# Attention and a grouped mixture of experts on one core: which 512 tokens go densely and when, sorting on GpSimd, results scattered by token

## The chip, the cores and the metric

One core of a Trainium2 chip runs the whole kernel. The time is device time in microseconds for one launch; the number compared is the median of several launches on the same chip. All arithmetic is in 32-bit floats, with small bf16 helpers. In the text the engines are called PE (TensorE, matmuls), DVE (VectorE), ACT (ScalarE), POOL (GpSimd) and SP (SyncE, which only issues DMAs here).

## The reference

Two batches of 1024 tokens, 128 features. First attention with latent keys and values, normed before and behind; then a mixture of experts, normed before and behind.

```
x = x + layernorm(attention(layernorm(x)))       # 8 heads, 2 latent kv heads of 32, causal
x = x + layernorm(ffn(layernorm(x)))

# ffn, per token h:
scores = sigmoid(h @ gate_weight.T)              # 32 experts in 4 groups of 8
sc     = scores + gate_bias
group_scores = top_k(sc.reshape(T, 4, 8), 2).sum(-1)
gidx   = top_k(group_scores, 2)                  # 2 of 4 groups stay open
topidx = top_k(sc where the group is open, 6)    # 6 experts
tw     = scores[topidx];  tw = tw / (sum + 1e-20) * 0.2
routed = sum over the 6 of tw * (silu(h @ w_gate[e]) * (h @ w_up[e])) @ w_down[e]
shared = (silu(h @ shared_w_gate) * (h @ shared_w_up)) @ shared_w_down
anchor = the same form with anchor topidx[:, 0] // 2
out    = routed + shared + 0.1 * anchor
```

Each token therefore needs 2 of the 4 groups; a group here holds 8 experts and 4 anchors and is computed as five chunks of 128 hidden columns.

## The kernel before

The 2048 tokens are four parts of 512: (batch 0, first half), (0, second), (1, first), (1, second). Three of them are sorted by group, so that only the two groups of each token are computed: their rows, 128 features and 48 weights (E + A), are written to the DRAM table `placed` at places given by `place_of`, in 15 slots of 256 rows (NS), of which each holds rows of one group. The fourth part, `dense`, goes through all four groups unsorted, with zero weights where a token has nothing to do with a group.

The sort has two sets. `place_first` (L971) covers the first two parts: `ranked` counts on PE how many earlier tokens chose each group, DVE works out the places (`slots_of`, `started`, `moved`), `numbers_of` (L949) reads the slots' group numbers into registers of PE and SP, and `move_rows` (L914) issues two indirect DMAs per tile of 128 tokens on POOL. `place_second` (L998) does it for the third part, which fills up what the first set left open.

All instructions stand in each engine's queue in the order in which the program writes them (`manual_schedule`), so an instruction that waits holds up everything behind it on its engine. Work beside the main line is written as generators: `tick()` (L251) advances one piece of each of the lists `ends`, `moves` and `side` by one step, and `yield HOP` makes a piece sit out two ticks. `attention()` ticks through its steps; `route` (L669), one generator for each part, does that part's output projection, the two norms, the router and the choice of groups and experts.

Behind attention comes `Slots.run` (L1146). For slot i and pair of chunks k it does `hidden` (gate and up matmuls, silu on ACT, two multiplies on DVE) and, two pairs later, `down`. At k = 0 it turns the rows of slot i+2 (`turn_rows`, L1067: four transposes, the weights written by ACT's queue to `cw_slot`) and fetches the weights of slot i+1; at k = 1 it fetches the rows of slot i+3 (L1062); at k = 2 the `spread` of slot i+2, the token weights of `cw_slot` broadcast over partitions (L1089, L1094). Weights, rows and spreads are all issued by SP, in this order. The result of a slot goes contiguously to `results` (L1141). When the slots are done, 24 indirect DMAs (`gather`, L1200) fetch the two results of each token, and `experts` (L1231) does the dense part, 20 chunks of 512 tokens, with `finish` (L1210: shared expert, sum, last norm, output) of the three sorted parts beside it in the ticks.

The norms' reciprocal root is always exp(-0.5 ln v) on ACT (`root`, L335) with a Newton step on DVE, and the router's sigmoid is a table of its own on ACT (L740), so that ACT loads tables at each change.

Of the kernel before, what the change touches and what calls it, by code (L numbers as in the profile page):

```python
# [17 lines left out]
P = 128  # L18
# [7 lines left out]
def attn_moe_block(  # L26
# [67 lines left out]

    sparse, dense = [(0, 0, TB), (0, TB, TB), (1, 0, TB)], [(1, TB, TB)]
    NT0 = 2 * TB
    NTS = sum(n for _, _, n in sparse)
    NS = TOPG * NTS * P // SL + NG - 1
    KS = NT0 * P // SL
    NS0 = -(-(TOPG * NT0 * P - NG * (SL - 1)) // SL)  # L100

# [66 lines left out]
    placed = dram.tile([NS * SL, D + E + A], F32, name="placed")  # L168
    results = dram.tile([NS * SL, D], F32, name="results")
    cw_slots = [dram.tile([E + A, SL], F32, name=f"cw_slot{i}") for i in range(NS)]  # L170
    cw_rows = {b: dram.tile([E + A, n * P], F32, name=f"cw_rows{b}") for b, _, n in dense}
# [8 lines left out]
    nc.gpsimd.memset(eps_t, EPS)  # L180
    ident_bf = const.tile([P, P], BF16, name="ident_bf")
# [29 lines left out]
    full = const.tile([P, NG, KS], F32, name="full")  # L211
    for k in range(KS):
        nc.gpsimd.memset(full[:, :, k], float(k * SL))
    number = const.tile([P, NS], F32, name="number")
    for i in range(NS):
# [3 lines left out]
    nc.gpsimd.memset(zero, 0.0)  # L219

# [4 lines left out]
    step_by = step_by.rearrange("p k g -> p (k g)")  # L225
    nc.sync.dma_start(
        out=placed.rearrange("(k p) c -> p k c", p=P),
        in_=zero.unsqueeze(1).to_broadcast([P, NS * JL, D + E + A]),
    )

# [17 lines left out]
    wakes, now = {}, 0  # L248
    HOP = 2

    def tick():  # L251
        nonlocal now
        now += 1
        for queue in (ends, moves, side):
            for piece in list(queue):
                if wakes.get(piece, 0) > now:
                    continue
                gap = next(piece, queue)
                if gap is queue:
                    queue.remove(piece)  # L260
                elif gap != 0:
                    wakes[piece] = now + (gap or 1)
                    break
# [57 lines left out]
    class Norm:  # L321
        def __init__(self, n, name):
            self.n = n
            for k, shape in (("st", [P, n, 6]), ("mv", [P, n, 2]), ("r0", [P, n]), ("t", [P, n]),
# [10 lines left out]
        def root(self):  # L335

            tables(EXP_LN)
# [3 lines left out]
        def newton(self):  # L341

# [4 lines left out]
            nc.vector.tensor_tensor(self.rs, r0, t, ALU.mult)  # L347

        def apply(self, dst, src, i):
            nc.vector.tensor_scalar(  # L350
                dst, src, self.mv[:, i, 0:1], self.rs[:, i : i + 1], ALU.subtract, ALU.mult
            )

        def negated(self):
            nc.vector.scalar_tensor_tensor(
                self.nb, self.mv[:, :, 0], -1.0, self.rs, ALU.mult, ALU.mult
# [23 lines left out]
    def project(b, c):  # L380
# [6 lines left out]
        yield  # L387
        if b:
            yield
        norm.root()  # L390
        yield
        norm.newton()
        if b:
            norm.negated()
            yield
        for i, t in enumerate(tiles):
            (norm.apply_act if b else norm.apply)(xn[:, i, :], x_sb[b][:, t, :], i)
        yield
        xnT = work.tile([P, BC], F32, tag="xnT", name=f"xnT{b}{c}")
        transposed(xn, xnT, f"xn{b}{c}")  # L400
        yield
# [261 lines left out]
    routed = {}  # L663
# [5 lines left out]
    def route(b, t0, n):  # L669


        name = f"{b}{t0}"
# [4 lines left out]
        sorts = (b, t0, n) in sparse  # L677
        assert n == TB
# [16 lines left out]
        norm.root()  # L695
        yield HOP
        norm.newton()
        norm.negated()
        yield HOP
# [9 lines left out]
        norm.root()  # L709
        yield HOP  # L710
        norm.newton()
        norm.negated()
        yield HOP
        if sorts:
            row = rows[b, t0] = const.tile([P, n, D + E + A], F32, name=f"rows{name}")
# [6 lines left out]
        yield HOP + 1  # L722
# [16 lines left out]
        loaded[0] = None  # L739
        nc.scalar.activation(score.rearrange("p t e -> p (t e)"), pl[:, 0 : n * E], AF.Sigmoid)  # L740
        yield HOP
        sc = scratch("sc", [E])
# [28 lines left out]
        if sorts:  # L771
            at = sum(p[2] for p in sparse[: sparse.index((b, t0, n))])
            own = chosen[:, at : at + n, :]
        else:
            own = gm
# [51 lines left out]
        if not sorts:  # L827
# [6 lines left out]
            nc.sync.dma_start(out=cw_rows[b], in_=cwT)  # L834
            yield
        routed[b, t0] = True
# [5 lines left out]


# [531 lines left out]
```

## Time and profile before

| | us |
|---|---|
| median of 4 launches | 508.68 (504.35 to 510.44) |
| the profiled launch | 507.35 |
| its span, first to last instruction | 505.6 |

| engine | busy us | share of the span | instructions |
|---|---|---|---|
| PE, matmuls | 429.2 | 85% | 3727 |
| DVE | 298.3 | 59% | 1046 |
| ACT | 222.0 | 44% | 464 |
| POOL | 83.7 | 17% | 160 |

The shares are means over stages that differ: attention, the slots, the dense part with the finishing of the others, and a tail. A line of the groups or of the timeline gives the engine, the line of the kernel, what is written and read with its partitions and elements, and a duration; what stands in brackets is the idle time of that engine just before, and what ended it. "issue" and "remote" are waits for which the profile finds no instruction or DMA of this kernel. The granted clock is PE's, as a share of full speed. An instruction that issues a DMA is charged to its queue (SPq, ACTq), not to the transfer.

### The profile page before, as it was taken

The numbers are of one execution on the slowest core, as the hardware profiler recorded it, in microseconds if no ns is written. First come the engines' busy times: TensorE is split into PE (matmuls) and PEld (weight loads), VectorE is DVE, ScalarE is ACT, GpSimd is POOL, SyncE is SP. The second block draws the span as 40 slices with busy tenths as digits, with TensorE's granted clock in tenths as the row PEclk, the third lists the DMA queues.
The fourth block names the chain that finished last, engine by engine and source line by source line (L and its number), as shares of the span: only waits on it lengthen the run. The fifth ranks groups of instructions, "written<-read, shape, count | busy, mean of one in ns | idle before, by whom it ended". The sixth has DMA issues, their size and how long they took to land.

```text
span 505.6 us, 10160 instructions
## 1 busy us (share of the span) xinstructions
PE 429.2 (85%) x3727; PEld 264.9 (52%) x3727; DVE 298.3 (59%) x1046; ACT 222.0 (44%) x464; POOL 83.7 (17%) x160
## 2 busy tenths in 40 slices
PE   8998979999889999859687479589989999937990
PEld 5554544545445556424334368578879874413430
DVE  4579563786967986986304554344665445416882
ACT  3445654566426765425436125434433222122442
POOL 3000000021001201003831005200000005750010
PEclk9999998999989999988759777899999999968996
DMA  8990000000000000001120725576677684624230
GB/s 221 209 273 10 2 1 2 1 2 3 2 1 2 3 1 1 2 1 67 66 80 8 218 90 161 146 210 212 186 239 223 194 272 113 162 64 134 60 89 21
DMA packets 42946, 47.45 MB, mean 94 GB/s; under 512 B 17392, under 2 KB 35936, under 8 KB 42896
## 3 DMA queue, kind: packets, MB, share of 16 engines
q1 hardware_dynamic: 37520, 39.81, 27.6%
q0 software_dynamic: 1920, 3.74, 2.5%
q10 hardware_dynamic: 3456, 3.25, 2.0%
q8 instruction: 30, 0.49, 0.4%
q14 instruction: 20, 0.16, 0.1%
HBM read 38.06 MB, written 11.34 MB: 98 GB/s over the span
## 4 chain that ended last, share of the span: by engine, by line
PE 46%; DVE 25%; issue 7%; DMA 6%; ACT 5%; POOL 4%; SPq 3%; another core or an unknown queue 1%; ACTq 0%; POOLq 0%; DVEq 0%
DVE nm L471 9%; DMA wbs<-wgu 5%; PE sm L454 5%; PE s L519 4%; PE pgs L1111 4%; PE ys L1134 4%; PE o L556 4%; PE pus L1111 3%; PE pp L407 3%; POOL placed L921 3%; PE o L565 3%; SPq L1094 2%; PE pg L1264 2%; PE pu L1265 2%; PE po L685 2%
## 5 line engine op out<-in xcount | busy, mean ns | idle before, releaser
L471 DVE TENSOR_REDUCE nm<-sm 128x1 f32<-128x512 f32 (+2 forms) x192 | 92.6, 548 | 47.3 <-PE sm L464 24.8
L539 ACT ACTIVATE pr<-s 128x512 f32<-128x512 f32 (+1 forms) x160 | 75.7, 558 | 81.0 <-PE s L533 72.0
L519 PE MATMUL s<-qT,kT 32*128 32x256 f32 (+1 forms) x640 | 54.0, 396 | 10.7 <-DVE pos L901 6.3
L519 PEld LDWEIGHTS s<-qT,kT 32*128 32x128 f32 x640 | 35.2, 190 | 28.6 <-issue 16.2
L1119 DVE TENSOR_TENSOR hids<-hids,pus 128x512 f32<-128x512 f32 x30 | 20.6, 687 | 49.6 <-PE pus L1111 38.6
L542 POOL TENSOR_SCALAR_AFFINE_SELECT pr<-pr 128x1024 f32<-128x1024 f32 x16 | 18.1, 1128 | 185.7 <-ACT pr L539 185.7
L556 PE MATMUL o<-pr,v 128*32 128x256 f32 (+1 forms) x640 | 43.1, 390 | 5.3 <-issue 3.9
L454 PE MATMUL sm<-kT,qT 32*128 32x512 f32 (+3 forms) x384 | 45.8, 533 | 1.5 <-DVE nm L471 1.2
L1134 PEld LDWEIGHTS ys<-wd_sb,hids 128*128 128x128 f32 x300 | 41.8, 199 | 5.3 <-DVE hids L1120 1.6
L565 PE MATMUL o<-pr,ones 128*32 128x256 f32 (+1 forms) x640 | 43.1, 369 | 1.6 <-issue 1.5
L1134 PE MATMUL ys<-wd_sb,hids 128*128 x300 | 42.5, 284 | 1.8 <-DVE hids L1120 1.2
L1203 POOL DMA_INDIRECT y<-results,place_of x24 | 23.0, 958 | 108.7 <-PE pu L1265 101.7
L1111 PE MATMUL pgs<-hTp,wbs 128*128 128x256 f32 x120 | 34.3, 412 | 7.7 <-DMA wbs<-wgu 5.5
L1118 ACT ACTIVATE hids<-pgs 128x512 f32<-128x512 f32 x30 | 17.9, 598 | 34.8 <-PE pgs L1111 34.7
L1111 PE MATMUL pus<-hTp,wbs 128*128 128x256 f32 x120 | 32.3, 393 | 0.0
L921 POOL DMA_INDIRECT placed<-rows,place_of x24 | 23.7, 989 | 51.2 <-DVE place_of L911 47.1
L556 PEld LDWEIGHTS o<-pr,v 128*32 128x32 f32 x640 | 17.5, 114 | 28.0 <-issue 18.2
L1268 ACT ACTIVATE hid<-pg 128x512 f32<-128x512 f32 x20 | 11.8, 597 | 46.0 <-PE pg L1264 25.7
L1269 DVE TENSOR_TENSOR hid<-hid,pu 128x512 f32<-128x512 f32 x20 | 13.7, 683 | 28.9 <-PE pu L1265 13.1
L565 PEld LDWEIGHTS o<-pr,ones 128*32 128x32 f32 x640 | 17.5, 110 | 24.6 <-issue 15.5
L1278 PE MATMUL oacc<-hid,wd_sb 128*128 128x512 f32 x40 | 21.8, 627 | 9.5 <-DVE hid L1270 9.5
L1120 DVE TENSOR_TENSOR hids<-hids,spreads 128x512 f32<-128x512 f32 (+1 forms) x45 | 27.1, 603 | 3.4 <-DMA spreads<-cw_slot 1.9
(270 smaller groups left out, 640.7 us busy)
## 6 DMA issues: line engine op xcount, KB each, us to landing
wbs<-wgu SPq DMA_DIRECT2D x15, 640.0 KB
spreads<-cw_slot SPq DMA_DIRECT2D x30, 256.0 KB
spreadd<-cw_rows SPq DMA_DIRECT2D x16, 256.0 KB
placed<-zero SPq DMA_DIRECT2D x1, 2640.0 KB
got<-placed SPq DMA_DIRECT2D x15, 176.0 KB
wbd<-wgu SPq DMA_DIRECT2D x4, 640.0 KB
spreads<-cw_slot SPq DMA_DIRECT2D x60, 32.0 KB
results<-ys ACTq DMA_DIRECT2D x15, 128.0 KB
```

What stands on the lines that cost most here:

```text
L454: nc.tensor.matmul(banks[r][:, at : at + k1 - k0], lhsT=qT[ts(r, L), g, ts(qt, P)], rhs=kT[ts(r, L), g, k0:k1], start=(at == 0), stop=Fals ...
L471: nc.vector.tensor_reduce(nm[:, k0 // BC, j, r : r + 1], banks[r][:, at : at + k1 - k0], AX.X, ALU.max, negate=True,)
L519: nc.tensor.matmul(banks[r][:, at : at + n], lhsT=kT[rows, g, ts(kt, P)], rhs=qT[rows, g, q * QC + lo : q * QC + lo + n], start=(i == 0), ...
L539: nc.scalar.activation(pr[:, r, 0:m], banks[r][:, 0:m], AF.Exp)
L556: nc.tensor.matmul(o[ts(r, L), lo : lo + n], lhsT=qkv[b][2][:, kt, ts(g, L)], rhs=pr[:, r, at : at + n], start=(kt == 0), stop=False, skip ...
L565: nc.tensor.matmul(o[ts(r, L), QC + lo : QC + lo + n], lhsT=ones32, rhs=pr[:, r, at : at + n], start=False, stop=True, skip_group_check=True,)
L921: move = nc.gpsimd.indirect_dma_start(out=placed[:, :], out_offset=bass.IndirectOffsetOnAxis(ap=place_of[:, k, i : i + 1], axis=0), in_=ro ...
L1111: nc.tensor.matmul(p[:, lo : lo + SL], lhsT=wb[:, m, ts(c, P)], rhs=hT, start=(lo == 0), stop=(c == pair[-1]), skip_group_check=True,)
L1120: nc.vector.tensor_tensor(hid[:, 0:n], hid[:, 0:n], sp[:, pair[0] : pair[-1] + 1, :].rearrange("p c t -> p (c t)"), ALU.mult,)
L1134: nc.tensor.matmul(o[:, ts(j, D)], lhsT=hid[:, at : at + P], rhs=w, start=(c == 0 and j == 0), stop=(c == NC - 1), skip_group_check=True,)
L1203: nc.gpsimd.indirect_dma_start(out=y[k][:, t, :], out_offset=None, in_=results[:, :], in_offset=bass.IndirectOffsetOnAxis(ap=place_of[:, k ...
L1278: nc.tensor.matmul(oacc, lhsT=wd_sb[:, c, :], rhs=hid, start=False, stop=(c == NG * NC - 1))
```

## The change

- The dense part is now the first part (batch 0, first half). It runs right behind attention, ahead of the slots. Parts 2 and 3 are the first set of the sort, part 4 the second.
- `place_first`, the first fetches of rows, the route of the last part and `place_second` are put on the list only when attention is over, and `tick` may then advance two side pieces at once (`at_once`). The first set's work thus runs beside the dense part.
- The arithmetic of the places moves from DVE to POOL, as more and smaller instructions (`more_than`, `in_turn`, `moved`). Registers with group numbers are now read by PE, SP and POOL.
- Each row in `placed` carries four more numbers: for each group, the row of `results` where this token's result for it belongs (twice the token's number, plus how many of its groups came before). Places that no token fills get spare rows. A slot's result is scattered to these rows by two indirect DMAs on POOL, and the 24 gathers give way to one plain read for each part (`finish`), in which a token's two results stand side by side.
- In `Slots.run` the rows of slot i+3 are fetched at k = 2, behind the spread of slot i+2, no longer at k = 1.
- `finish` of parts 2 to 4 runs beside the slots; the last one has to wait for the last slot. Parts 2 and 3 wait for 11 slots (NB0).
- Outside attention the norms' roots are taken on POOL with `pow` (`root_pool`); in attention the router's sigmoid is made from exp, so that ACT keeps its table.

The diff, cut to its core:

```diff
-    sparse, dense = [(0, 0, TB), (0, TB, TB), (1, 0, TB)], [(1, TB, TB)]
+    parts = [(b, t, TB) for b in range(B) for t in range(0, NT, TB)]
+    ND = 1
+    sets = [parts[1:3], parts[3:]]
+    NB0 = TOPG * NT0 * P // SL + NG - 1
+    ROW = D + E + A + NG
...
-    results = dram.tile([NS * SL, D], F32, name="results")
+    results = dram.tile([NTS * P * TOPG + NS * SL, D], F32, name="results")
...
+    nc.sync.dma_start(out=by_place[:, :, D + E + A : ROW], in_=spare)
...
-        for queue in (ends, moves, side):
+        for queue, most in ((ends, 1), (moves, 1), (side, at_once[0])):
...
+        def roots(self):
+            if loaded[0] == EXP_LN:
+                self.root_act()
+                yield HOP
+                self.newton()
+            else:
+                self.root_pool()
+            yield HOP
...
+        def root_pool(self):
+            eng, v, t, r0 = nc.gpsimd, self.v, self.t, self.r0
+            eng.tensor_scalar(v, self.var, EPS, None, ALU.add)
+            eng.tensor_tensor(r0, v, minus_half.to_broadcast([P, self.n]), ALU.pow)
...
+        if in_attention:
+            nc.scalar.activation(flat, pl[:, 0 : n * E], AF.Exp, scale=-1.0)
...
+        if sorts:
+            below = preceded[:, at : at + n, :]
...
+            nc.gpsimd.tensor_tensor(
+                row[:, :, D + E + A : ROW], below,
+                token_row[:, at : at + n].unsqueeze(2).to_broadcast([P, n, NG]), ALU.add,
+            )
...
+    def more_than(dst, x, n):
+        t = tiny("more", [P, NG])
+        eng.tensor_scalar(dst, x, 0.0, None, ALU.is_gt)
+        for k in range(1, n):
+            eng.tensor_scalar(t, x, float(k * SL), None, ALU.is_gt)
+            eng.tensor_tensor(dst, dst, t, ALU.add)
+
+    def in_turn(start, first, n):
+        eng.tensor_copy(start, first)
+        for d in range(1, NG):
+            eng.tensor_tensor(start[:, d:NG], start[:, d:NG], n[:, 0 : NG - d], ALU.add)
...
     def place_first():
...
+        more_than(full, far, NT0 * P // SL)
+        more_than(new, total, NT0 * P // SL)
...
+        in_turn(starts[:, 0, :], nslots.to_broadcast([P, NG]), full)
...
+        in_turn(starts[:, 1, :], nslots.to_broadcast([P, NG]), new)
...
+        moved(0, NT0, rank, "a")
         moves.append(move_rows(0, NT0, "first"))
+        routed.add(("first", "placed"))
+        yield HOP + 1
+        yield from numbered(0, NS0)
...
         def begin(self):
-            while "first" not in routed:
+            while ("first", "moved") not in routed:
                 yield 0
-            self.fetch_weights(0)
             for i in range(3):
                 self.fetch_rows(i)
...
+            while "experts fetched" not in routed:
+                yield 0
+            self.fetch_weights(0)
...
         def turn_rows(self, i):
...
+            nc.gpsimd.tensor_copy(
+                self.to_row[i].unsqueeze(2), got[:, :, D + E + A : ROW][:, :, bass.ds(self.groups[i], 1)]
+            )
...
         def down(self, i, k, hid):
...
                 nc.scalar.copy(y, o[:, 0 : JL * D])
-                nc.scalar.dma_start(
-                    out=results[ts(i, SL), :].rearrange("(p j) d -> p j d", j=JL),
...
+                for j in range(JL):
+                    nc.gpsimd.memset(between, 0.0)
+                    move = nc.gpsimd.indirect_dma_start(
+                        out=results[:, :],
+                        out_offset=bass.IndirectOffsetOnAxis(ap=self.to_row[i][:, j : j + 1], axis=0),
+                        in_=y[:, ts(j, D)], in_offset=None,
+                    )
...
         def run(self):
...
                     if k == 0:
                         self.turn_rows(i + 2)
                         self.fetch_weights(i + 1)
-                    if k == 1:
-                        while NS0 <= i + 3 < NS and "second" not in routed:
-                            tick()
-                        self.fetch_rows(i + 3)
                     if k == 2:
                         self.fetch_spread(i + 2)
+                        self.fetch_rows(i + 3)
-                    for _ in range(1 if "second" in routed else 3):
+                    for _ in range(3):
                         tick()
...
+    def finish(i):
...
+        while some.done < (NS if last else NB0):
+            yield 0
...
+        nc.sync.dma_start(
+            out=both.rearrange("p (t c) -> p t c", t=n),
+            in_=results[0 : NTS * P * TOPG, :].rearrange("(t p k) d -> p t (k d)", p=P, k=TOPG)[
+                :, at : at + n, :
+            ],
+        )
...
-    some = Slots()
-    side += [*(route(*part) for part in sparse[:2]), place_first(), some.begin()]
-    side += [*(route(*part) for part in sparse[2:]), place_second()]
-    side += [route(*part) for part in dense]
-    attention()
-    some.run()
-    for b, t0, n in dense:
...
+    side += [route(i) for i in range(len(parts) - 1)]
+    attention()
+    at_once[0] = 2
+    some = Slots()
+    side += [place_first(), some.begin(), route(len(parts) - 1), place_second()]
+    experts(0, 0)
+    side += [finish(i) for i in range(ND, len(parts))]
+    some.run()
```

## The prediction

> **What bounds the kernel now.** I read the page's slices first, then a table by stage, then the waits, then the timeline of two places. The slices (each digit a fortieth of the span, in tenths) show TensorE (PE) near full in attention and ragged behind it, with the granted clock falling there.
>
> ```profile
> PE   8998979999889999859687479589989999937990
> PEclk9999998999989999988759777899999999968996
> ```
>
> By stage (window, its length, then busy time and count of PE, weight loads, DVE, ACT, POOL; granted clock, DMA share, GB/s):
>
> ```profile
> 220.50:226.70 6.20, 0.00 (x0) 0.00 (x0) 5.44 (x30) 1.42 (x3) 0.00 (x0) 0.77 0.00 0
> ...
> 246.70:266.00 19.30, 13.21 (x82) 5.14 (x80) 1.19 (x3) 6.42 (x13) 9.58 (x17) 0.56 0.23 76
> ...
> 273.00:337.10 64.10, 45.01 (x229) 38.53 (x229) 29.43 (x120) 25.92 (x55) 10.29 (x21) 0.84 0.51 151
> 337.10:415.50 78.40, 74.32 (x469) 68.28 (x470) 44.67 (x131) 28.88 (x62) 0.00 (x0) 1.00 0.73 217
> 415.50:493.40 77.90, 65.02 (x154) 27.96 (x153) 43.96 (x98) 23.77 (x38) 26.79 (x27) 0.91 0.39 109
> 493.40:505.60 12.20, 0.66 (x4) 0.42 (x4) 2.92 (x16) 2.95 (x5) 1.26 (x1) 0.64 0.07 22
> ```
>
> Attention ends at 273, the 15 slots at 415.5, the dense part at 493.4; 12.2 us of tail follow. PE sets the time where it is fed, and it is not fed in four places: 220.5 to 226.7, 246.7 to 266, the first slots, and parts of the dense stage. The waits (total us, times, longest):
>
> ```profile
> ACT pr L539 <- remote: 7.9, 2, 7.1
> ...
> DVE hid L1269 <- remote: 7.4, 1, 7.4
> ...
> PE s L519 <- DVE pos L901: 6.3, 1, 6.3
> ```
>
> The last one is the hole at 220.5: PE's queue holds the register loads of `numbers_of` (L950), which need DVE's 30 small instructions of `place_first`. The two "remote" waits lie at 251 and 443, each while POOL issues indirect DMAs back to back (twelve from 242.9, then 24 gathers from 421.5); PE, ACT and DVE stand together with no releaser in the kernel.
>
> **The change, part by part.** *Attention.* `place_first` and its 16 moves leave it. Gone: the 6.2 us hole, and in 246.7 to 266 the difference between 19.3 us and 13.21 us at clock 0.56 (7.4 us of full-clock work), 11.9 us; some 2 us of clock lost behind the first hole (20 us at 0.90) too. One unit more of routing is moved in (four transposes and a copy for the dense part, five small POOL instructions for each sorted one): 1 us. Sum -19: attention ends at 254. If the 11.9 us have another cause than the moves, it is 266.
>
> *Dense part, now first.* The same 20 chunks: PE starts pairs of L1264 at 423.45 and 426.03, so 20 x 2.57 = 51.4, plus 2.1 for the shared matmuls (1.02 + 1.12) and 2 for the last two chunks: 55.5. The 24 gathers and the 8.5 us that PE stood in them (442.9 to 451.4) are gone. Its weights and first spreads have nothing before them on SP and load during attention. Beside it runs now the sorting, on POOL. I count 35 + 15 = 50 small POOL instructions in `place_first` (`more_than` twice 7, `in_turn` twice 4), then 16 moves, 27 small ones and 8 moves in `place_second`, and 16 in the two `root_pool` of the last part's route. Of POOL (group, busy us, mean ns) the trace shows:
>
> ```profile
> L921 POOL DMA_INDIRECT placed<-rows,place_of x24 | 23.7, 989 | 51.2 <-DVE place_of L911 47.1 <-issue 3.8
> ...
> L920 POOL MEMSET between<- 128x1 f32 x24 | 2.7, 112 | 0.0
> ...
> L201 POOL TENSOR_TENSOR rep<-rep,ident 128x32 f32<-128x32 f32 x2 | 0.5, 242 | 0.0
> ```
>
> The 128x4 arithmetic is not in it, nor `pow`: between 0.11 (a memset) and 0.24 us each; I take 0.20, nearer to the only arithmetic. A move costs 0.99 + 0.11 + 0.19 of issue = 1.27 us. From the end of attention: the third part's route ends some 6 ticks in, at 1.29 us each (two in a chunk) behind 4 us of start, and five ticks later the counts are there: 18. Then 50 x 0.20 = 10, 16 x 1.27 = 20.3, the route's own POOL work of 5 (two adds of 0.73, 16 root steps, memsets): 53. Rows back (2.4), turned, cut to `cw_slot` and spread (6 to 8): a first slot at 62 to 64. So POOL's chain (63) is longer than PE's work (55.5). POOL is in order: the last route's adds and roots queue behind the moves, ACT and DVE wait for them, and behind those stand the silu and the multiplies of the chunks. SP waits for the last move with later spreads queued behind it. I add 6 to the 63 for that and for a standstill as at 443 (8.5 us of PE), of which part falls into waits that exist anyway, and 1.3 for registers (225.4 to 226.7 before): 70, against 77.9 before. Ends: 57 (all hidden) and 85 (both standstills and all waits in series).
>
> A rule speaks against this: the Trainium skill, "GPSIMD Engine Reference", section 4.1, sends elementwise work to VectorE and calls GpSimd about twice as slow for two inputs. The 128x4 multiply of DVE (L347) took 0.162 us, and by that rule the 50 would cost 0.32 each and the stage 6 us more: 487 instead of 481.
>
> *The slots.* One edit decides here. `fetch_rows(i+3)` moves on SP from before `fetch_spread(i+2)` to behind it. That spread needs `cw_slot`, which needs the rows of i+2 turned. SP waited for just this:
>
> ```profile
> SPq L1089 <- DMA cw_slot<-cwTs: 39.0, 11, 16.2
> ```
>
> One round in the timeline (start, us, engine, line):
>
> ```profile
> 333.03 0.38 PE L1072 MATMUL pt_s<-ident,got 128*128 128x128 f32 x2
> ...
> 333.67 0.36 ACT L1078 COPY cwTs<-pt_s 48x256 f32<-48x256 f32 x1 [1.59 <-PE pt_s L1074]
> ...
> 334.06 0.32 ACTq L1079 DMA_DIRECT2D cw_slot<-cwTs  x1
> ...
> 335.76 1.16 SPq L1089 DMA_DIRECT2D spreads<-cw_slot  x2
> ...
> 337.12 2.36 SPq L1094 DMA_DIRECT2D spreads<-cw_slot  x4
> ...
> 339.73 0.40 SPq L1025 DMA_DIRECT2D wbs<-wgu  x1
> ...
> 340.92 0.42 SPq L1062 DMA_DIRECT2D got<-placed  x1
> ```
>
> And what a row read takes when somebody waits for it:
>
> ```profile
> 320.88 0.35 SPq L1062 DMA_DIRECT2D got<-placed  x1
> ...
> 323.24 0.69 PE L1072 MATMUL pt_s<-ident,got 128*128 128x128 f32 x2 [5.24 <-DMA got<-placed]
> ```
>
> Before, rows(i+3) did not wait for spread(i+2), so the round (turn, copy, `cw_slot`, spread, rows, turn) had two slots to close. After it has one: turn to `cw_slot` issue 1.03, landing 1.70 here (3.9 at 341.78 with weights in flight), spread issue 3.5 to 3.7, row read 2.36, 0.2 of gaps: 8.8 to 11.2. Weights are issued right behind the rows, 3.4 us ahead of the next `cw_slot`, so I take a landing of 2.3: 9.5 us a slot. Before, the copies L1140 at 351.87 and 412.44 are eight slots apart, 7.57 each; PE's own work is some 7.0. From slot 2's turn (2.9 into the slots) to slot 14's: 12 x 9.5 = 114, and 17.6 of PE behind it: 134.5, against 142.4 (415.5 - 273). The shared matmuls of `finish` (3 x 2.2) fit into PE's gaps of 2.5. Two scatters a slot are 2.5 us of POOL in 9.5, hidden; the second set's places are ready near slot 2, where rows(5) ask for them: 0 to 4, inside the round.
>
> *Tail.* From the last matmul: copy 0.5, two scatters 2.4, landing 1.5 (257.81 to 259.29 at the first rows), the read of both results 4.3 (640 KB of weights took 5.0), two adds 1.4, statistics 1.25, roots 1.7, applying 1.0, add 0.7, the output 5.1 (500.5 to 505.6): 20 against 12.2. The dense part's own tail is covered by slots now.
>
> *The rest* costs nothing seen: the 16-byte spare columns are written in the first 45 us and read after 254; `to_row` is one POOL copy a slot; the sigmoid from exp saves two table loads of 1.28 us on ACT in attention, where PE sets the pace.
>
> Sum: 254 + 70 + 134.5 + 20 = 478.5, +1.75 around the span (507.35 - 505.6) = 480; the median of 508.68 is 1.3 above the profiled run, so **481**.
>
> **Rivals.** *The row round does not close late* (turns find their rows): 7.5 x 15 = 112.5 in place of 134.5, 459. For it: in the trace only one turn ever waited for rows. Against: there rows ran a slot ahead. *The round is longer*: `cw_slot` lands in 3.9 as at 341.78, or PE's gap passes some 3 us and the clock drops, as behind the 3.5 us gap at 299.6 (not behind 2.2 at 274): 11.2 a slot, +20, 501. *The standstill at 246.7 was not the moves'*: attention ends at 266, 492. *Slower: POOL is the bound.* If a small POOL instruction costs 1 us (`pow` and 128x4 are unseen), the 50 put 40 us in front of the first slot, the roots 13 more, the second set 10 in the slots: some 530 with part hidden; it decides from 0.6 us each, where the 27 us gained are used up.
>
> **How the numbers follow.** Forecast 0.38 (its own range 466 to 495), rows on time 0.17, standstill stays 0.09, longer round 0.18 (half of it below 503.6), POOL the bound 0.18. A measurement here tells 1% from nothing, so faster (below 503.6) is 0.38 + 0.17 + 0.09 + 0.09 = 0.73, within 0.08 + 0.02 = 0.10, slower 0.17. 452 to 517 leaves out 0.04 of the fast case and most of the slow one.
>
> **What would show it.** Right: attention over near 254 without the hole at 220; from the third slot on PE waits for `got` before each turn, with slots 9 to 10 us apart and SP's rows behind its spreads; a tail near 20. Wrong: slots 7.5 apart; PE standing in the dense part behind POOL for over 20 us; POOL instructions of 128x4 far above 0.24.

## The result, and the profile after

The changed kernel takes 507.65 us (median of 42 runs, 502.53 to 510.81), the kernel before 507.36 (63 runs, 502.83 to 518.59). The ratio is 1.0006 with an interval of 0.9987 to 1.0024: no difference. The profiled execution after is 510.93 us with a span of 509.2, 0.6% above the median. Ratios and intervals leave out runs over 1.5% above the fastest of the same kernel, which medians keep; the traces of the changed kernel (510.93), of the moves apart (524.16) and of the reads on POOL (486.46) are of such runs.

One thing has to be known for every number below. The kernel before has two times. In three of the five sets of runs made for the experiments (kernels run one after the other on one chip; four chips in all, sets 1 and 2 on the same one) it took 508 us, as in the comparison above; in the other two it took 478 and 481, without exception within a set. The changed kernel took 508 to 509 in a set of either kind. Beside a kernel before of 481 us the change is 6% slower.

The slices of the page, PE's busy share and the granted clock in fortieths of the span, show no hole towards the end of attention, where before has two (220.5 and 246.7). There is one in slice 23, in the dense part (PE at 3), and a hollow in slices 27 to 29, where the slots begin, with the clock at 6 in slice 29:

```profile
PE   8998899998799999997999379976797978788760
PEclk9997999999799999999999779998688989899885
```

The table by stage (window, length, busy time and count of PE, weight loads, DVE, ACT, POOL; clock, DMA share, GB/s): attention, the dense part, the slots up to the copy of slot 3's result out of PSUM (slots counted from 0), the other slots, the tail.

```profile
0.00:254.00 254.00, 235.04 (x2868) 127.27 (x2869) 179.15 (x687) 132.03 (x298) 30.19 (x91) 0.97 0.19 48
254.00:330.70 76.70, 64.17 (x175) 29.25 (x176) 39.73 (x132) 26.17 (x46) 41.84 (x120) 0.91 0.41 118
330.70:395.30 64.60, 49.15 (x232) 40.62 (x231) 21.30 (x45) 16.98 (x38) 24.08 (x62) 0.84 0.46 135
395.30:491.90 96.60, 80.52 (x456) 71.46 (x454) 44.88 (x90) 26.97 (x62) 32.62 (x67) 0.93 0.59 173
491.90:509.20 17.30, 0.00 (x0) 0.00 (x0) 4.56 (x18) 3.04 (x6) 2.19 (x5) 0.64 0.17 57
```

Set against the forecast's sum, in its own terms:

| term | forecast | measured |
|---|---|---|
| attention ends | 254 | 254.0 |
| dense part | 70 | 76.7 |
| to slot 2's turn | 2.9 | 1.6 |
| slot 2's turn to slot 14's, 12 rounds | 114 | 134.3 |
| from there to the last copy | 17.6 | 25.3 |
| tail | 20 | 17.3 |
| span | 478.5 | 509.2 |

The turns of slots 2, 6 and 14 stand in the timeline of PE:

```profile
332.30 0.38 PE L1113 MATMUL pt_s<-ident,got 128*128 128x128 f32 x2
...
390.74 0.68 PE L1113 MATMUL pt_s<-ident,got 128*128 128x128 f32 x2 [3.05 <-DMA got<-placed]
...
466.58 0.44 PE L1113 MATMUL pt_s<-ident,got 128*128 128x128 f32 x2 [2.47 <-DMA got<-placed]
```

The first four rounds took 58.4 us where 38 were forecast, the eight behind them 75.8 where 76 were. So the first four are 20.4 of the 30.7 us by which the sum was too small; the stretch behind the last turn is 7.7, the dense part 6.7, and the other terms give 4.2 back. Two more traces of the changed kernel (`c1_after` and `c2_after`, 508.07 and 508.45) have 56.5 and 56.8 for the four rounds, 76.5 and 75.3 for the eight. Slot 3's copy (395.3) falls near slot 6's turn, and is used below as another mark of where the beginning ends.

The waits between 254 and 331 (total us, times, longest):

```profile
DVE hid L1329 <- ACT hid L1328: 17.7, 3, 13.4
ACT an L398 <- POOL between L963: 13.0, 1, 13.0
...
PE oacc L1338 <- DVE hid L1330: 8.7, 2, 8.6
```

They are one chain, read from its second line: ACT's normalising step of the last route waits 13.0 us for POOL (the releaser shown, a memset, is what POOL does next after the root); the silu L1328 stands behind it on ACT, the multiply behind the silu, PE behind the multiply. The timeline of POOL (start, duration) shows what POOL was doing:

```profile
280.45 0.96 POOL L964 DMA_INDIRECT placed<-rows,place_of  x1 [0.19 <-issue]
281.49 0.23 POOL L383 TENSOR_SCALAR v_attn<-mv_attn 128x4 f32<-128x4 f32 x1
281.80 1.06 POOL L384 TENSOR_TENSOR r_attn<-v_attn,minus_half 128x4 f32<-128x4 f32 x1
...
284.07 0.20 POOL L389 TENSOR_TENSOR t_attn<-mv_attn,rs_attn 128x4 f32<-128x4 f32 x1
284.36 0.24 POOL L390 TENSOR_SCALAR nb_attn<-t_attn 128x4 f32<-128x4 f32 x1
```

The root came behind 15.6 us of place arithmetic (261.4 to 277.0) and three moves. In the slots' beginning the same happens with the dense part's own last norm, and SP is held as well (waits from 331 to 400):

```profile
ACT y L398 <- POOL between L963: 13.8, 1, 13.8
DVE y L393 <- POOL rs_out L388: 10.0, 1, 10.0
```

POOL itself was held up there. It did the place arithmetic of the second set (328.7 to 336.6) and three moves, and the fourth move waited for the row read of slot 3; the root came behind it, at 347.76:

```profile
345.24 0.96 POOL L964 DMA_INDIRECT placed<-rows,place_of  x1 [4.65 <-DMA got<-placed]
```

That read had itself waited for moves. SP's queue there: the row read of slot 3 leaves at 342.14, 2.3 us behind the end of the spread's issue, that of slot 4 at 361.95, 3.5 us behind.

```profile
337.54 2.27 SPq L1139 DMA_DIRECT2D spreads<-cw_slot  x4
342.14 0.35 SPq L1103 DMA_DIRECT2D got<-placed  x1
...
356.47 1.99 SPq L1139 DMA_DIRECT2D spreads<-cw_slot  x4
361.95 0.35 SPq L1103 DMA_DIRECT2D got<-placed  x1
```

In the steady slots the round runs as forecast; from slot 6 on the turns come 9.1 to 9.8 us apart. SP issues the spread, then the rows, and PE's turn waits for them; the next spread leaves only behind the turn:

```profile
414.12 1.99 SPq L1139 DMA_DIRECT2D spreads<-cw_slot  x4
416.21 0.36 SPq L1103 DMA_DIRECT2D got<-placed  x1
...
419.60 0.44 PE L1113 MATMUL pt_s<-ident,got 128*128 128x128 f32 x2 [0.74 <-DMA got<-placed]
...
422.38 1.16 SPq L1134 DMA_DIRECT2D spreads<-cw_slot  x2
```

These waits of PE over the whole run, before (total us, times, longest):

```profile
PE pt_s L1072 <- DMA got<-placed: 5.2, 1, 5.2
```

and after:

```profile
PE pt_s L1113 <- DMA got<-placed: 20.3, 11, 3.3
```

### The profile page after: what moved, and what is told of

The parts are those of the page before. It is cut to its first block, busy times and chain, and to the rows that moved or that the text cites. A ratio compares the mean times of both kernels' runs of the same rounds, so it can differ in the third digit from the quotient of the medians.

```text
span 509.2 us, 10254 instructions
## 1 busy us (share of the span) xinstructions
PE 428.9 (84%) x3727; PEld 268.6 (53%) x3727; DVE 289.6 (57%) x970; ACT 205.2 (40%) x449; POOL 130.9 (26%) x343
## 4 chain that ended last, share of the span: by engine, by line
PE 37%; DVE 21%; DMA 14%; POOL 9%; issue 6%; SPq 6%; ACT 5%; POOLq 1%; ACTq 0%; DVEq 0%
DVE nm L508 8%; PE sm L491 7%; DMA got<-placed 6%; PE s L556 4%; PE o L593 4%; SPq L1139 4%; PE o L602 3%; POOL placed L964 3%; PE pp L444 3%; PE pgs L1156 2%; PE pus L1156 2%; DMA cw_slot<-cwTs 2%; SPq L1134 2%; DMA placed<-rows,place_of 2%; DVE parts L524 1%
## 5 line engine op out<-in xcount | busy, mean ns | idle before, releaser
L556 PE MATMUL s<-qT,kT 32*128 32x256 f32 (+1 forms) x640 | 51.3, 391 | 6.1 <-DVE nm L508 4.5
L491 PE MATMUL sm<-kT,qT 32*128 32x512 f32 (+3 forms) x384 | 47.9, 548 | 0.2 <-ACT qT L445 0.2
L1179 PEld LDWEIGHTS ys<-wd_sb,hids 128*128 128x128 f32 x300 | 43.7, 206 | 6.7 <-issue 2.5
L1179 PE MATMUL ys<-wd_sb,hids 128*128 x300 | 44.0, 291 | 3.1 <-DVE hids L1165 2.1
L1188 POOL DMA_INDIRECT results<-ys,to_row x30 | 31.8, 1059 | 53.6 <-ACT ys L1185 42.7
L1156 PE MATMUL pgs<-hTp,wbs 128*128 128x256 f32 x120 | 36.0, 428 | 4.1 <-DVE shf L1226 3.3
L602 PE MATMUL o<-pr,ones 128*32 128x256 f32 (+1 forms) x640 | 39.4, 364 | 0.0
L1156 PE MATMUL pus<-hTp,wbs 128*128 128x256 f32 x120 | 35.8, 427 | 0.0
L1156 PEld LDWEIGHTS pus<-hTp,wbs 128*128 128x128 f32 x120 | 26.3, 220 | 4.7
L964 POOL DMA_INDIRECT placed<-rows,place_of x24 | 25.1, 1045 | 9.2 <-DMA got<-placed 4.7
```

Source lines behind the costliest of these rows:

```text
L491: nc.tensor.matmul(banks[r][:, at : at + k1 - k0], lhsT=qT[ts(r, L), g, ts(qt, P)], rhs=kT[ts(r, L), g, k0:k1], start=(at == 0), stop=Fals ...
L556: nc.tensor.matmul(banks[r][:, at : at + n], lhsT=kT[rows, g, ts(kt, P)], rhs=qT[rows, g, q * QC + lo : q * QC + lo + n], start=(i == 0), ...
L602: nc.tensor.matmul(o[ts(r, L), QC + lo : QC + lo + n], lhsT=ones32, rhs=pr[:, r, at : at + n], start=False, stop=True, skip_group_check=True,)
L964: move = nc.gpsimd.indirect_dma_start(out=placed[:, :], out_offset=bass.IndirectOffsetOnAxis(ap=place_of[:, k, t : t + 1], axis=0), in_=ro ...
L1156: nc.tensor.matmul(p[:, lo : lo + SL], lhsT=wb[:, m, ts(c, P)], rhs=hT, start=(lo == 0), stop=(c == pair[-1]), skip_group_check=True,)
L1179: nc.tensor.matmul(o[:, ts(j, D)], lhsT=hid[:, at : at + P], rhs=w, start=(c == 0 and j == 0), stop=(c == NC - 1), skip_group_check=True,)
```

## The experiments

All times are medians; "pitch" is the distance of two slots' copies out of PSUM (L1185 of the changed kernel, or its counterpart), "the first four rounds" the time from slot 2's turn to slot 6's.

| set | before | the kernels beside it, with the ratio to before and its interval |
|---|---|---|
| 1 | 478.11 | rows early 486.92, 1.0154 (1.0094 to 1.0215); roots on ACT 506.86, 1.0590 (1.0524 to 1.0655); places on DVE 502.75, 1.0484 (1.0417 to 1.0550); before with late rows 497.82, 1.0370 (1.0296 to 1.0443) |
| 2 | 507.83 | before 508.91; changed 509.26, 1.0006 (0.9970 to 1.0042); free rows 500.61, 0.9848 (0.9814 to 0.9881); four edits 489.04, 0.9635 (0.9612 to 0.9659) |
| 3 | 480.87 | changed 508.47, 1.0598 (1.0484 to 1.0712); three edits 478.81, 0.9981 (0.9937 to 1.0025); reads on POOL 481.50, 1.0022 (0.9975 to 1.0069); late shared 504.59, 1.0490 (1.0363 to 1.0617) |
| 4 | 507.75 | six edits 489.58, 0.9641 (0.9587 to 0.9694); before 508.07; five edits 491.56, 0.9665 (0.9598 to 0.9733) |
| 5 | 508.87 | before with a memset more 508.35, 0.9976 (0.9938 to 1.0013); three edits again 482.13, 0.9498 (0.9435 to 0.9561); moves apart 518.38, 1.0111 (1.0024 to 1.0199) |

As the changed kernel takes 507.65, 509.26 and 508.47 in three comparisons of both kinds, kernels made from it are set against 508.5 where it was not in the same set.

**Rows early** (the row read ahead of the spread again):

```diff
-                        self.fetch_spread(i + 2)
                         self.fetch_rows(i + 3)
+                        self.fetch_spread(i + 2)
```

> The changed kernel with one edit: the rows of slot i+3 are fetched on SP ahead of the spread of slot i+2, as the kernel before had it. Theory (the row round is what sets a steady slot): matmuls of steady slots come some 7.5 us apart instead of 9.3 to 9.7, about ten slots x 2 = 20 us off the slots, so about 488 us; PE's waits for got before a turn go from 20.3 us in 11 to near nothing. Rival (the rows are only the last of several that come at the same time: the weights, the landing of cw_slot, the silus): pitch stays above 9 and the time stays within 1% of 507.

486.92, 21.6 us less. Most pitches are 7.0 to 7.6 until slot 11, with 8.8 to 9.1 now and then; PE's waits for `got` fall from 20.3 us to 1.0. Slot 3's copy to slot 13's takes 81.9 us (93.5 in the changed kernel), and the beginning is shorter too: slot 3's copy comes 53.6 us into the slots instead of 61 to 65, and the first four rounds take 49.3 instead of 56.5 to 58.4. The timeline shows the order turned round: rows at 411.55, the turn at 419.21 with no wait ahead of it.

```profile
411.55 0.35 SPq L1103 DMA_DIRECT2D got<-placed  x1
...
415.35 1.19 SPq L1134 DMA_DIRECT2D spreads<-cw_slot  x2
...
419.21 0.38 PE L1113 MATMUL pt_s<-ident,got 128*128 128x128 f32 x2
```

The waits of PE for rows in this run:

```profile
PE pt_s L1113 <- DMA got<-placed: 1.0, 2, 0.8
```

**The same edit alone, on the kernel before** (the read of slot i+3 moves from k == 1 to behind the spread at k == 2):

```diff
-                        self.fetch_rows(i + 3)
                     if k == 2:
                         self.fetch_spread(i + 2)
+                        self.fetch_rows(i + 3)
```

> The kernel before with one edit of the change: the rows of slot i+3 are fetched on SP behind the spread of slot i+2. Theory (this edit alone lengthens a steady slot from 7.57 to about 9.5 us): about eleven slots x 1.9 = 21 us more, a ratio of 1.03 to 1.05 to the kernel before, with PE waiting for got before its turns. Rival (the pitch of 9.5 in the changed kernel comes from its other edits: scatters, 16 more bytes a row, the sorted second set, the cast on GpSimd): ratio within 1% of 1.

497.82 beside 478.11: 19.7 us. The pitch from slot 3 to slot 13 is 9.07 on average, against 7.57 in the trace of before, and PE waits 23.1 us in 9 for `got`:

```profile
PE pt_s L1072 <- DMA got<-placed: 23.1, 9, 8.3
```

From both sides this one edit is worth some 20 us.

**Roots off GpSimd** (behind attention too, `roots` loads the table, takes logarithm and exponential on ACT, and the rest on DVE):

```diff
-            if loaded[0] == EXP_LN:
+            if True:
+                tables(EXP_LN)
                 self.root_act()
```

> The changed kernel with the roots of the norms behind attention taken off GpSimd: a logarithm and an exponential on ScalarE (with the tables loaded for them) and four instructions on VectorE. Theory (silus and multiplies of the dense part and of the first slots stood behind roots that queued on GpSimd behind place arithmetic and moves): the 8.55 us and 3.04 us stands of PE near 280 and 296 go, the dense part takes 66 to 69 us instead of 76.9, and the waits of 13.8 us (ACT) and 10.0 us (DVE) near 337 to 351 go, 4 to 8 us more: about 492 to 497 us. Rival (something else is late in the same places: the moves, the spreads, the clock): the dense part stays at 74 or more and the time within 1% of 507.

506.86, 1.6 less: a miss. The 8.55 us stand became 3.27, but at 303 PE stood 5.22 us at the first turn for rows, and the dense part ended at 330.2 as before. The root was one of several things late there; the next was the rows that PE turns, and they wait for the moves.

**Place arithmetic on VectorE**:

```diff
-    eng = nc.gpsimd
+    eng = nc.vector
```

> The changed kernel with the arithmetic of ranked, place_first and place_second on VectorE instead of GpSimd; the moves and the roots stay on GpSimd. Theory (GpSimd is late because of its 50 small instructions, 15.6 us): the first set's moves begin 8 to 10 us sooner, the root that PE waits for at 288.55 comes about 8 us sooner, the second set's moves end by about 345 instead of 356.6; 5 to 12 us less, about 495 to 502. Rival (VectorE, 50% busy in the dense part, loses what GpSimd gains, its multiplies queueing behind 77 more instructions): no change within 1%, or slower.

502.75, 5.8 less. The arithmetic of the first set took 8.7 us (265.45 to 274.16) instead of 15.6, the dense part ended at 325.45 instead of 330.1 to 330.8.

**Free rows** (reads of slots 3 and 4 join the group of moves that do not wait for one another):

```diff
+                if 3 <= i < NS0:
+                    tc.declare_no_dep(read.ins, group="placed", reason="the second set writes behind these")
+                    tc.add_to_no_dep_group("placed", read.ins)
```

> The changed kernel, where the reads of the rows of slots 3 and 4 do not wait for the moves of the second set (those slots hold first-set rows only). Theory (SP stood 11.6 us at rows(3) and more at rows(4) for moves that write elsewhere, with weights and spreads behind it): SP's waits at the row reads go from 17.3 us to about 6, slots 0 to 3 take 8 to 12 us less, time about 497. Rival (the same slots wait for GpSimd's root and for spreads anyway): less than 4 us.

500.61 beside 509.26 for the changed kernel: 8.7 less. The read of slot 3 left at 340.02, directly behind its spread; slot 3's copy came 55.5 us into the slots, against 60.9, and the first four rounds took 48.5, against 56.5. The edit frees the moves from the reads as well: the fourth move of the second set no longer waits (341.08), and the root behind it begins at 342.50 instead of 347.76. How much of the 8.7 is the reads and how much the root was not taken apart.

**Late shared matmuls** (`finish` first waits for slots):

```diff
+        while some.done < 2 + i:
+            yield 0
         yield 3
```

> The changed kernel with one edit: the shared matmuls of finish for the three sorted parts begin after 3, 4 and 5 slots instead of in the first slots. Theory (the first slots are long because PE, ACT and VectorE carry them there, and VectorE's part stands behind the root of the dense part's norm): slot 3's copy comes 6 to 10 us sooner after the start of the slots (61 to 64 us now), and as later slots have gaps that the matmuls fit into, 4 to 8 us less in all. Rival (the first slots wait for the second set's rows whatever else they hold): within 2 us.

504.59 beside 508.47: 3.9 less, slot 3's copy 57.0 us in against 61.2, the first four rounds 51.4 against 56.8. With four runs of each (500.61 to 507.87 and 507.03 to 511.89) the 3.9 is not a sharp number. The size was overrated: PE now stands 4.1 us at 341 with no releaser shown, probably behind its own register loads (see six edits), and 4.7 at 355 for the copy of slot 0.

**Four edits** (the first, roots, places, free rows) and **three** (without the roots), the latter in two sets:

> The changed kernel with four edits together: rows fetched ahead of the spread, roots behind attention off GpSimd, place arithmetic on VectorE, and rows of slots 3 and 4 not waiting for the second set's moves. Theory: what the four give by themselves adds up for the most part, the round 20 us, places on VectorE 5, the other two some 5: about 475 us, near the kernel before on a chip where that has no standstill. Rival (they hide one another): not below 485, the value of the first edit alone.

> The changed kernel with three edits: rows ahead of the spread, place arithmetic on VectorE, rows of slots 3 and 4 free of the second set's moves; the roots stay on GpSimd. Theory (the fourth edit, roots by ScalarE, costs what it frees: table loads and a longer chain): 482 to 487 us, below the 489.04 of all four. Rival (the roots on ScalarE were worth something): above 489.

> The three edits again (rows ahead of the spread, place arithmetic on VectorE, rows of slots 3 and 4 free), which took 478.8 where the kernel before took 480.9. Theory: as its trace shows no standstill, it takes 477 to 483 here whatever the kernel before takes: a ratio near 0.945 beside 508, near 1 beside 478. Rival: beside a kernel before of 508 it takes 487 to 491, as the runs of four, five and six edits did.

489.04 with the roots on ACT, where 475 was expected; 478.81 and 482.13 without. The edit that gave nothing alone costs 7 to 10 here (the two were not in one set). The three edits add up to 36 by themselves (21.6 + 5.8 + 8.7) and give 30 in the same set as the changed kernel (508.47 - 478.81). Beside a kernel before of 508.87 the three edits are 5% faster, beside one of 480.87 level. Slot 3's copy lies 48.8 us into the slots, and the first four rounds take 44.5 (44.7 in the second set).

**Reads on POOL** (three edits, and the reads of the first two sorted parts issued by POOL):

```diff
-        nc.sync.dma_start(
+        (nc.sync if last else nc.gpsimd).dma_start(
             out=both.rearrange("p (t c) -> p t c", t=n),
```

> The three edits of the run before and a fourth: the reads of the results for the first two sorted parts are issued by GpSimd, which wrote them, instead of SP. Theory (SP stood 11 us at these reads for scatters, with the last slots' weights and spreads behind it; the slot in which that falls took 13.8 instead of 7 us): 6 to 10 us less than the run before. Rival (GpSimd, in order, then holds the last scatters back as long): no gain.

481.50 beside 478.81: the rival. POOL waits for the data it has asked for (waits from 440 to 470), a root queues behind it, and PE stands behind that:

```profile
POOL results L1191 <- DMA y<-results: 11.0, 1, 11.0
ACT shared L398 <- POOL nb_out L390: 11.0, 1, 11.0
...
PE ys L1182 <- DVE hids L1168: 8.1, 1, 8.1
```

**Six and five edits** (the three; the dense part's last norm after three slots; the adds of the results after 9 ticks instead of 4; six has the late shared matmuls as well):

```diff
-            yield HOP
+            while some.done < 3:
+                yield 0
             yield from normed(f"out{b}{u}", b, u * TB, own)
```

> The changed kernel with six edits: rows ahead of the spread, place arithmetic on VectorE, rows of slots 3 and 4 free of the second set's moves, the dense part's last norm after three slots instead of at once, the adds of the results five ticks later, the shared matmuls of finish after 3, 4 and 5 slots. Theory: PE's 6.36 us stand behind VectorE and GpSimd's root near 338 and the 13 us slot near 450 go, so slot 3's copy comes 42 to 44 us after the slots' start instead of 48.8, and the time is 466 to 472 us, below the kernel before in either of its times (478 and 508). Rival (the delayed work comes back later, in the last slots or the tail): 476 to 481.

> The same as the run of six edits, but with the shared matmuls of finish in the first slots as in the changed kernel. Theory: PE has the shared matmuls' 6.6 us to do in either place and is near full in both, so within 3 us of the run of six. Rival (they hold the first slots up as they did when moved alone, 4 us): 3 to 5 us above the run of six.

489.58 and 491.56, 7 to 13 us above the three edits, which ran in other sets. Six misses its 466 to 472; that five lies within 3 us of six came as expected. The trace of six is of its quickest run, 484.41. In it slots 1 and 2 come at 7.0 and 7.7, but the norm and the shared matmuls come back at slots 3 to 5 with pitches of 14.3, 10.2 and 10.2. And PE's stand near 338, which I had put down to the norm's root, is still there in the timeline of PE, now without a data wait:

```profile
337.80 2.04 PE L1159 MATMUL pgs<-hTp,wbs 128*128 128x256 f32 x4 [7.25 <-issue]
```

PE issues register loads there, whose numbers come from `numbered` of the second set; VectorE has them ready at 334.87, and SP, which reads them too, goes on at 337.51. That these loads hold PE, as at 220.5 in the kernel before, is the likely reading; it was not tried by itself.

**The kernel before, and its two times.** It was run for a trace (`c0_before`, `c3_before`), with one memset more (`f2_twice`), and the changed kernel beside it (`c1_after`, `c2_after`):

> The kernel before, unaltered, with a trace from a chip on which it takes 478 us instead of 507 (the four runs ahead of this one were on such a chip). Theory: the standstills of PE, ACT and DVE at 246.7 to 266 and near 443, which the trace of 505.6 us shows without a releaser, are absent here, worth about 12 + 8 us and some clock. Rival: every stage is shorter by the same share (a quicker clock all over), and the standstills remain.

> The changed kernel, unaltered, on the same chip as the others of this call. Theory (the standstills belong to a chip and hit the kernel before alone, as the changed kernel's trace shows none): 505 to 510 us here too, and a ratio of 1.05 to 1.07 to the kernel before if that takes 478. Rival (the chip makes both faster): ratio within 1.5% of 1.

> The changed kernel, unaltered, once more, because the kernel before took 478 us in the first four runs here and 508 us in the next four. Theory: the kernel before has two times, by the standstills of its moves and gathers, and the changed kernel has one: it takes 505 to 511 us whichever the kernel before takes. Rival: what lengthens the kernel before lengthens the changed one too, and where the kernel before takes 478 this one takes some 480.

> The kernel before, unaltered, for a trace of an execution of 478 us. Theory: no standstill without a releaser at 246.7 to 266 nor at 443, attention over near 262 instead of 273, the pitch of slots 7.5 as in the trace of 505.6 us. Rival: the same standstills, and all stages shorter. (If it takes 508 again, it tells neither.)

> The kernel before with one memset of 128x1 more at its start and nothing else, for a trace of an execution of 478 us, if it takes that here. Theory: then no standstill without a releaser near 247 to 258 nor near 443, attention over near 262, the slots' pitch 7.5. Rival: at 478 the same standstills, with all else shorter. At 508: the standstills as in the trace of 505.6 us.

`c1_after` 509.26 and `c2_after` 508.47: the changed kernel has one time, the kernel before two. None of the three traces of before fell in a set where it took 478; all took 508 and show the standstills at the same two places: ACT waits 3.4 to 4.9 us near 250 and 7.1 near 257, VectorE 8.2 to 18.0 us up to 450, with no releaser. The only trace of this order from a set of 478 is that of the late rows in set 1. There twelve moves go out back to back as before (from 243.27), and the stretch from 246.7 to 266 has no standstill (clock 0.98 instead of 0.56), attention ends at 260.8 instead of 273, and the dense part takes 66.3 us (420.3 to 486.6) instead of 77.9:

```profile
246.70:266.00 19.30, 13.14 (x190) 7.80 (x191) 6.24 (x45) 12.88 (x27) 11.09 (x25) 0.98 0.25 79
```

12.2 and 11.6 are 24 of the 30 us between the two times. What decides between the two stays open: the chip does not (sets 1 and 2 ran on the same one), nor does it change within a set. Fetching of instructions is an obvious rival, but in none of the four traces of before does the DMA view show an instruction fetch between 246.7 and 262 or between 441 and 452.

**Moves apart** (the kernel before, with four ticks between two moves):

```diff
                 tc.add_to_no_dep_group("placed", move.ins)
-                yield
+                yield 4
```

> The kernel before with its moves further apart: four ticks instead of one between two of them. Theory (the standstill at 246.7 to 266 comes with moves back to back): beside a kernel before of 508, no such standstill in attention, the first slots later for the moves' sake, 498 to 506; beside one of 478, later first slots alone, 480 to 490. Rival (the moves do not cause it): beside 508 the standstill remains at its place and the time is 508 or more.

518.38 (512.14 to 524.16) beside 508.87. The theory's 498 to 506 did not come; the time is the rival's, "508 or more", but not its place. 246.7 to 261 is now undisturbed but for one wait of 1.0 us. The next six moves went out back to back from 262.39 on all the same, behind an instruction of POOL that had waited 13.75 us, and the standstill came with them (timeline):

```profile
266.20 0.96 POOL L921 DMA_INDIRECT placed<-rows,place_of  x1 [0.19 <-issue]
...
267.47 0.96 POOL L921 DMA_INDIRECT placed<-rows,place_of  x1 [0.19 <-issue]
...
268.73 0.96 POOL L921 DMA_INDIRECT placed<-rows,place_of  x1 [0.19 <-issue]
269.59 0.58 ACT L572 COPY raw<-o 128x512 f32<-128x512 f32 x1 [8.57 <-remote]
```

In this one trace it went with the moves, not with the old place. The other standstill, at the gathers, is longer here than in the first trace (VectorE waits 16.1 us instead of 7.4), which is part of why the time rose. Moves alone do not make it: four of them from 242.26 to 246.08 here and eleven from 280.36 on, the twelve in the trace of the late rows, and the 16 of the changed kernel beside the dense part, show none.

## Why the prediction was wrong

**Attention: right.** Over at 254.0, no hole at 220, no standstill. That the standstill goes with moves fits the run with the moves apart. What could not be seen in one trace is that it is not always there: beside a kernel before of 478, attention gains 7 us (260.8 - 254.0, by the trace of the late rows), not 19. And near 443 the three engines did not all stand: of the 8.5 us from 442.9 ACT worked 3.7 (a silu, two table loads, a root).

**Dense part: the mechanism right, the size short by 6.7.** "POOL is in order: the last route's adds and roots queue behind the moves, ACT and DVE wait for them, and behind those stand the silu and the multiplies" is what the waits show, 8.55 and 3.04 us of PE. The "6" that I gave it covered half. The 50 small instructions took 15.6 us instead of 10: one 128x4 takes the 0.20 that I took, but one follows the other only every 0.31 us. The standstill that I feared here did not come.

Here the rule of the Trainium skill ("GPSIMD Engine Reference", section 4.1), that GpSimd is about twice as slow for two inputs, has to be read with care. The trace has 0.20 against 0.162 us for a single 128x4 instruction, a factor of 1.2; but the whole chain of dependent instructions took 15.6 us on GpSimd and 8.7 on VectorE, a factor of 1.8. The rule's price for the chain, 6 us more, was nearer than mine.

**Slots: this is the step that failed**, the term "From slot 2's turn (2.9 into the slots) to slot 14's: 12 x 9.5 = 114, and 17.6 of PE behind it: 134.5". The round of 9.5 is right for eight of the twelve: slot 6's turn to slot 14's took 75.8 (8 x 9.5 = 76), PE waits for `got` before its turns, and the edit that I said decides is worth some 20 us from both sides. But I used the steady round from slot 2's turn on, and the first four took 58.4 (56.5 and 56.8 in two more traces) instead of 38. The trace of before showed what they cost there: 55.0 for the first four, 62.3 for the eight behind them.

```profile
278.00 0.38 PE L1072 MATMUL pt_s<-ident,got 128*128 128x128 f32 x2
...
333.03 0.38 PE L1072 MATMUL pt_s<-ident,got 128*128 128x128 f32 x2
...
395.35 0.38 PE L1072 MATMUL pt_s<-ident,got 128*128 128x128 f32 x2
```

In copies: slot 3's came 63.7 us into the slots before, and comes 64.6 in now (61.2 in a second trace). I wrote "0 to 4, inside the round" for the second set and that the shared matmuls "fit into PE's gaps"; neither held in the first slots. One edit at a time brings the first four rounds from 56.5 to 58.4 down to 48.5 (reads of slots 3 and 4 and moves of the second set that waited for one another), 49.3 (late rows) and 51.4 (shared matmuls in the first slots). The three overlap: the first two, with the places on VectorE, leave 44.5. What makes the 6.5 that are still above 38 was not taken apart.

The other size in this term, "17.6 of PE behind it", was short as well: 25.3 here, and 20.2 in the trace of before (395.35 to 415.53). SP issues two reads of the results at 466.22 there, ahead of the last slot's spread (473.27) and weights (477.20), and PE stands 2.10 us for a multiply and 0.81 for these weights. That the reads cost the 7.7 is not shown; issuing them on POOL brought nothing.

**Tail: right in kind**, 17.3 for 20.

**The rivals.** Rows on time is excluded by the turns, 9.1 to 9.8 apart; the rival that keeps the standstill (attention over at 266) is excluded by attention's end at 254.0; POOL the bound at 0.6 us an instruction did not come (0.20, or 0.31 with the gap). The longer round (501) came nearest to the time, but by luck: the steady rounds were not longer, the first four were.

**So the gain went back.** Beside a kernel before of 508, attention gave 19 and the dense part 1; the slots took 18.7 (161.2 for 142.5) and the tail 5 of it. That leaves 3.6, by which the two traced runs differ; the medians differ by 0.3. Beside one of 478, 12 of the 19 us were not there to be had, the dense part was already some 10 us shorter than the changed kernel's (66.3 in the trace of the late rows), and 28 us are lost (508.47 - 480.87).

## What to carry to other kernels

A steady pitch holds for steady slots: take the first ones from the trace of before by themselves, as far as the pitch is not yet reached. A read that is moved on its queue behind an instruction that waits for the round before can turn a two-stage round into one of a single stage; here that cost 1.5 to 1.7 us in every steady slot (7.57 to 9.07 in the kernel before; 7.58 to 9.27 up to slot 11 in the changed one), whatever the engines had free. And work sent to an idle in-order engine queues everything else on that engine: ask what its next waiting customer is, and whose instructions stand behind that one.

## What the runs showed that was not expected

- The same program took 478 or 508 us, fixed within a set of runs and different between sets on the same chip. The traces put 24 of the 30 us on two places where engines stand 3.4 to 18 us at a time during runs of indirect DMAs. A gain that consists in removing such a stall exists only where the stall does. Its cause was not found.
- Dependent small instructions (most of 128x4) on GpSimd follow one another every 0.31 us although most are shown with 0.20 to 0.25; on VectorE every 0.17. `pow` on 128x4 took 1.05 us.
- A DRAM table written by row made the reads of the rows of slots 3 and 4 wait for moves into other rows, and a move wait for such a read, with a norm's root behind it: 8.7 us that no datum required.
